# Two graph layers in fp32 on one core: the seven products of a block-matrix unit in three PSUM banks instead of five

## The chip, the cores and the metric

One Trainium2 chip, of which the kernel uses one core. The metric is the device time in microseconds of one execution; the profile is one further execution of the same program, recorded by the hardware profiler. All arithmetic is fp32.

## The reference, cut to what matters

64 graphs of 256 nodes with 512 features pass through two layers that share one 256x256 adjacency matrix. Layer 0 is masked multi-head attention (8 heads of 64), layer 1 a graph attention with one score per pair of nodes. Each layer normalises its input, clips it at zero and adds its result to the input.

```
h = jnp.maximum(_layernorm(x, axis=-1), 0.0)
# layer 0
q, k, v = ((h @ W + b).reshape(b, n, H, HD) for W, b in ...)
scores = jnp.einsum('bqhd,bkhd->bhqk', q, k) / jnp.sqrt(jnp.float32(HD))
scores = scores + (1.0 - adj)[None, None, :, :] * -1000000000.0
out = jnp.einsum('bhqk,bkhd->bqhd', softmax(scores), v).reshape(b, n, d)
x = x + out @ Wo + bo
# layer 1
h = jnp.maximum(_layernorm(x, axis=-1), 0.0)
g = jnp.einsum('bnc,cf->bnf', h, W)
e = leaky_relu(s1[:, :, None] + s2[:, None, :], 0.2) * adj     # s1, s2 = g @ a1, g @ a2
x = x + elu(einsum('bij,bjf->bif', softmax(e), g) + beta * g)
```

## The kernel before, in words

The graphs are worked through in 32 **pairs**. The five matrix products with a 512x512 weight (queries and keys, values, output projection, layer 1) are taken over the two graphs of a pair and over two halves of the weight, as a 2x2 block product with seven block products instead of eight (the Winograd form of Strassen). One such set of seven is a `Unit`: `UnitQK` (two per pair, `ua` and `ub`), `UnitV`, `UnitO`, `UnitW`. A product `P1` to `P7` is eight matmuls into one PSUM bank (128x512). The four results of a unit are called by graph and half: (0,0), (0,1), (1,0), (1,1). With U2 = P1+P6 and U3 = U2+P7 they are P1+P2, U2+P5+P3, U3+P4 and U3+P5.

In the kernel before, `Unit.p` gives P1 (`a`), P4 (`d`), P5 (`b`), P6 and P7 (`k`) a bank each; only P2 is added by TensorE into `a`, and P3 into `b`. ScalarE copies P1 into an SBUF tile `u2` (line 278), VectorE adds P6 to it (280) and P7 into `u3` (283). `put11`, `put2` and `put12` write the results: for queries and keys with the bias (364, 369), for values 398 to 405, for the output projection 490 (into the residual tile `y`, to which GpSimd has added U2 or U3 before, `ahead`, 486), for layer 1 through `elu` (599, 600, 609) and `finish` (614, 615). P3 is accumulated into the bank `b` that `put2` reads for (1,1), so P3 follows that read.

The instructions of TensorE, VectorE, ScalarE and GpSimd run in the order in which the program text issues them; each engine works through its own queue in that order. Only SyncE's queue of DMAs is ordered by the framework. The main loop has two functions per pair p: `first_half` (the values of pair p, then for pair p-2 the layer-1 product, for pair p-1 most of the output projection) and `second_half` (its end, the transposes `x_t` of pair p+1, attention of the two graphs, queries and keys of pair p+1). `v_chain` is the start of `first_half` and holds the softmax of layer 1 of pair p-2: scores (`gat_scores`, 528, 530), exponential (535), division (540, 542), transposes (551). `o_blocks` (460), `combine_2` (299) and `combine_4` (303) form the operand sums of a unit. The first pair and the last ones have texts of their own (`start`, `first`, `last`, `end`).

The residual tiles `y` have six buffers. `residual` loads one (467) and GpSimd adds the bias (468). Four belong to pair p-2 until line 609 has read them, two to (0,0) and (1,1) of pair p-1; so the tile (1,0) of pair p-1 takes the buffer that (0,0) of pair p-2 leaves, and the tile (0,1) the one that (1,1) leaves.

```
    BUFS = {"set": 13, "qk": 8, "v": 4, "pt": 8, "x": 4, "y": 6, "e": 2, "eT": 2, "m": 2, "c": 3, "u": 4}
...
        r = Y[g, fh] = blk(tag, f"y_{g}_{fh}")
        nc.sync.dma_start(r, x[g].rearrange("(t p) c -> p t c", p=P)[:, :, fh * N:(fh + 1) * N])
        nc.gpsimd.tensor_tensor(r, r, bo2[:, fh * N:(fh + 1) * N].unsqueeze(1).to_broadcast([P, 2, N]), ALU.add)
```

## Time and profile before

| | |
|---|---|
| device time, median of 3 runs | 2898.32 us (2898.24 to 2899.57) |
| profiled execution | 2898.09 us, span 2896.3 us, granted TensorE clock 0.999 |
| TensorE busy | 2818.8 us, 97% of the span |
| VectorE, ScalarE, GpSimd busy | 70%, 36%, 57% |
| DMA | 110.00 MB, mean 38 GB/s |

The span runs from the first to the last instruction; about 1.8 us of the execution lie outside it. In the views of instructions, a row gives line, engine, operation, the tiles written and read, shape and count, then the busy time and the mean duration of one, then the idle time of the engine just before such instructions and who ended it. In a timeline a row gives start and length in us, and in square brackets the idle time ahead of it and the engine and tile that ended it. PE is TensorE, DVE VectorE, ACT ScalarE, POOL GpSimd, SPq the DMA queue of SyncE. Matmuls overlap in the records: eight of one product start 0.216 us apart and each is shown some 0.38 us long.

### The profile page before, as it was taken

Reading aid. Unit: us, or ns where it says so; the run is one execution under the profiler, and the core shown is the slowest. Engines: PE = TensorE matmul, PEld = TensorE weight load, DVE = VectorE, ACT = ScalarE, POOL = GpSimd, SP = SyncE. Lnnn points to the kernel's source line nnn. Section 1 sums busy time; section 2 is a strip of 40 time slices with the busy share of each in tenths; the row PEclk is TensorE's granted clock in tenths of the full one; section 3 lists DMA queues with packets and bytes.
Section 4 is the critical chain, followed back from the end, with each engine's and each line's share of the span. In section 5 each row is a group of like instructions: output and inputs, shape, how many; then the busy total and the mean of one; then the engine's idle time right before and its main releaser. Section 6 shows DMA issues by size and latency. Waiting matters only on the chain.

```text
span 2896.3 us, 46339 instructions
## 1 busy us (share of the span) xinstructions
PE 2818.8 (97%) x18110; PEld 2344.3 (81%) x18110; DVE 2035.7 (70%) x3678; ACT 1041.7 (36%) x2122; POOL 1647.2 (57%) x1564
## 2 busy tenths in 40 slices
PE   9999999999999999999999999999999999999997
PEld 7788888888888888888888888888888888888875
DVE  6766766677766767666776667776677766677677
ACT  3233333333343333333333333334333333333324
POOL 3655555556464664645555555646466464555574
PEclk9999999999999999999999999999999999999999
DMA  5010011100111001111001110011100111101111
GB/s 150 5 37 23 30 44 44 44 17 28 44 45 45 29 24 37 44 45 36 24 30 44 45 44 17 29 44 45 44 27 25 37 44 44 34 26 30 37 34 41
DMA packets 96479, 110.00 MB, mean 38 GB/s; under 512 B 8576, under 2 KB 79488, under 8 KB 96256
## 3 DMA queue, kind: packets, MB, share of 16 engines
q1 hardware_dynamic: 96256, 106.99, 11.9%
q8 instruction: 145, 2.38, 0.3%
q14 instruction: 78, 0.64, 0.1%
HBM read 73.41 MB, written 33.55 MB: 37 GB/s over the span
## 4 chain that ended last, share of the span: by engine, by line


## 5 line engine op out<-in xcount | busy, mean ns | idle before, releaser
L422 POOL TENSOR_TENSOR pt<-pt,maskT 128x512 f32<-128x512 f32 x512 | 705.8, 1378 | 663.3 <-ACT pt L421 663.3
L424 POOL TENSOR_TENSOR pp<-pt 128x256 f32<-128x256 f32 x512 | 417.1, 815 | 40.1
L421 ACT ACTIVATE pt<-sc 128x512 f32<-128x512 f32 x512 | 257.6, 625 | 473.5 <-PE sc L417 473.5
L446 DVE RECIPROCAL rec<-sm 128x256 f32<-128x256 f32 x128 | 224.3, 1752 | 73.8 <-PE sm L444 73.8
L518 DVE SCALAR_TENSOR_TENSOR pr<-h,war 128x512 f32<-128x512 f32 x256 | 265.4, 1080 | 0.0
L435 PE MATMUL av<-pt,v 128*32 128x256 f32 x4096 | 246.0, 381 | 0.2 <-DVE v L405 0.2
L417 PE MATMUL sc<-qk 64*128 64x256 f32 x2048 | 238.5, 383 | 0.0
L417 PEld LDWEIGHTS sc<-qk 64*128 64x128 f32 x2048 | 193.1, 187 | 46.0 <-issue 13.5
L564 PE MATMUL pz<-eT,h 128*128 128x256 f32 x1024 | 226.8, 379 | 1.9 <-ACT eT L552 1.9
L614 POOL TENSOR_TENSOR o<-o,m 128x512 f32<-128x512 f32 x29 | 37.0, 1275 | 318.2 <-ACT m L600 307.3
L564 PEld LDWEIGHTS pz<-eT,h 128*128 128x128 f32 x1024 | 194.4, 190 | 28.9 <-ACT eT L552 2.6
L435 PEld LDWEIGHTS av<-pt,v 128*32 128x32 f32 x4096 | 126.6, 110 | 98.4 <-issue 21.5
L486 POOL TENSOR_TENSOR y<-y,o_u 128x512 f32<-128x512 f32 x93 | 126.7, 1377 | 90.1 <-DVE o_u L280 82.6
L535 ACT ACTIVATE e<-e 128x256 f32<-128x256 f32 x128 | 52.2, 409 | 322.5 <-DVE e L530 322.5
L468 POOL TENSOR_TENSOR y<-y,bo 128x512 f32<-128x512 f32 x128 | 161.4, 1283 | 0.0
L567 ACT COPY z<-pz 128x512 f32<-128x512 f32 x128 | 74.9, 587 | 190.3 <-PE pz L564 190.3
L542 DVE SCALAR_TENSOR_TENSOR e<-e,grec,betai 128x256 f32<-128x256 f32 x128 | 137.5, 1112 | 2.3
L351 PE MATMUL qk_p<-h,wq_b 128*128 128x256 f32 x512 | 134.7, 386 | 0.2 <-ACT h L328 0.2
L512 ACT ACTIVATE h<-y,nmr_y,rstd_y 128x256 f32<-128x256 f32 x256 | 132.5, 591 | 1.1
L351 PE MATMUL qk_p<-h,wk_t 128*128 128x256 f32 x512 | 131.5, 379 | 0.0
L351 PE MATMUL qk_p<-h,wq_t 128*128 128x256 f32 x512 | 131.5, 379 | 0.0
L351 PE MATMUL qk_p<-s_h,wq_t 128*128 128x256 f32 x512 | 131.4, 379 | 0.0
(171 smaller groups left out, 6082.2 us busy)
## 6 DMA issues: line engine op xcount, KB each, us to landing
x<-in_x_dram SPq DMA_DIRECT2D x128, 256.0 KB, 2.8
y<-in_x_dram SPq DMA_DIRECT2D x128, 256.0 KB, 2.9
out_dram<-o SPq DMA_DIRECT2D x116, 256.0 KB, 2.6
out_dram<-y SPq DMA_DIRECT2D x11, 256.0 KB, 2.1
wq_b<-in_L_gnn_Wq_dram SPq DMA_DIRECT2D x4, 256.0 KB, 5.8
wk_b<-in_L_gnn_Wk_dram SPq DMA_DIRECT2D x4, 256.0 KB, 6.1
wv_b<-in_L_gnn_Wv_dram SPq DMA_DIRECT2D x4, 256.0 KB, 4.9
wo_b<-in_L_gnn_Wo_dram SPq DMA_DIRECT2D x16, 64.0 KB, 2.5
```

What stands on the lines that cost most here:

```text
L351: nc.tensor.matmul(ps[:, j * N:(j + 1) * N], wj[i][:, c, ft * P:(ft + 1) * P], s[i][:, c, :], start=(start and j == 0 and c == 0), stop=(c ...
L417: nc.tensor.matmul(pss[2 * pair + h][:, k * N:(k + 1) * N], qk[hs, 1, k * P:(k + 1) * P], qk[hs, 0, :], start=True, stop=True)
L421: nc.scalar.activation(pt, two(pss[i]), AF.Exp, scale=QSCALE)
L422: nc.gpsimd.tensor_tensor(pt, pt, maskT, ALU.mult)
L424: nc.gpsimd.tensor_tensor(pp, pt[:, 0, :], pt[:, 1, :], ALU.add)
L435: nc.tensor.matmul(ps[i * HH:(i + 1) * HH, s * N:(s + 1) * N], v[:, k, c0:c0 + HH], pts[i][:, k, :], start=(k == 0), stop=(k == NT - 1))
L446: nc.vector.reciprocal(rec, sums[:, :N])
L468: nc.gpsimd.tensor_tensor(r, r, bo2[:, fh * N:(fh + 1) * N].unsqueeze(1).to_broadcast([P, 2, N]), ALU.add)
L512: nc.scalar.activation(h2[t][:, f * N:(f + 1) * N], Y[g, f][:, t, :], AF.Relu, bias=nmr[:, t:t + 1], scale=rstd[:, t:t + 1])
L518: nc.vector.scalar_tensor_tensor(pr, H2[g][t], 1.0, war[:, j, :], op0=ALU.mult, op1=ALU.mult, accum_out=SC[g][:, t, j:j + 1])
L542: nc.vector.scalar_tensor_tensor(e[:, t, :], e[:, t, :], rec[:, t:t + 1], betai[:, (1 - t) * P:(3 - t) * P], op0=ALU.mult, op1=ALU.add)
L564: nc.tensor.matmul(ps[:, f * N:(f + 1) * N], h2[k][:, fs], eT[:, k, :], start=(k == 0), stop=(k == NT - 1))
```

## The change

P1, P6, P7 and P4 are accumulated one after the other into one bank `a`. After P1, P6 and P7 ScalarE copies the running sum into SBUF (`u1`, `u2`, `u3`), and the next of the four products follows that copy. P2 has the bank `c` to itself, P5 and P3 the bank `b`. VectorE's additions of lines 280 and 283 are gone; (0,0) is now P2 plus `u1` on VectorE, and (1,0) is read straight from `a`. The order of the products in a unit becomes 1, 2, 6, 5, 7, then 4 and 3, with products of another unit, or transposes, between; `queries` interleaves the two units of queries and keys. GpSimd's `ahead` of the output projection remains for (0,0) and (0,1). In `first_half`, `o_blocks` stands earlier, and the second pair of residual loads stands after P7 of `UnitW`. The buffer counts stay. `start`, `first`, `last` and `end` are rewritten to the same scheme, the last `UnitW`s lose their variant with sums on ScalarE and GpSimd (`pooled`), and the last unit has P3 in a bank of its own (`p_34`). The core of the diff:

```diff
-            if i in (2, 3):
-                self.mm(i, self.a if i == 2 else self.b, False)
-                return
-            ps = bank(f"{self.name}_p{i}")
-            setattr(self, {1: "a", 4: "d", 5: "b", 6: "k", 7: "k"}[i], ps)
-            self.mm(i, ps, True)
-            if i == 1:
-                self.u2 = blk("u", f"{self.name}_u2")
-                nc.scalar.copy(self.u2, two(ps))
-            if i == 6:
-                nc.vector.tensor_tensor(self.u2, two(ps), self.u2, ALU.add)
-            if i == 7:
-                self.u3 = blk("u", f"{self.name}_u3")
-                nc.vector.tensor_tensor(self.u3, two(ps), self.u2, ALU.add)
+            if i in (1, 2, 5):
+                setattr(self, {1: "a", 2: "c", 5: "b"}[i], bank(f"{self.name}_p{i}"))
+            ps = {1: "a", 6: "a", 7: "a", 4: "a", 2: "c", 5: "b", 3: "b"}[i]
+            self.mm(i, getattr(self, ps), i in (1, 2, 5))
+            if i in (1, 6, 7):
+                u = blk("u", f"{self.name}_u{i}")
+                setattr(self, {1: "u1", 6: "u2", 7: "u3"}[i], u)
+                nc.scalar.copy(u, two(self.a))
...
-        def put11(self):
-            dst, bias = self.new(0, 0)
-            for j in range(2):
-                nc.scalar.activation(dst[:, j, :], self.a[:, j * N:(j + 1) * N], AF.Identity, bias=bias[j])
-
         def put(self, gi, fh, ps, u):
             dst, bias = self.new(gi, fh)
             for j in range(2):
                 nc.vector.scalar_tensor_tensor(dst[:, j, :], ps[:, j * N:(j + 1) * N], bias[j], u[:, j, :],
                                                op0=ALU.add, op1=ALU.add)
 
-        def put2(self):
+        def put11(self):
+            self.put(0, 0, self.c, self.u1)
+
+        def put22(self):
             self.put(1, 1, self.b, self.u3)
-            self.put(1, 0, self.d, self.u3)
+
+        def put21(self):
+            dst, bias = self.new(1, 0)
+            for j in range(2):
+                nc.scalar.activation(dst[:, j, :], self.a[:, j * N:(j + 1) * N], AF.Identity, bias=bias[j])
 
         def put12(self):
             self.put(0, 1, self.b, self.u2)
...
-            nc.scalar.copy(self.new(0, 0), two(self.a))
-
-        def put2(self):
+            nc.vector.tensor_tensor(self.new(0, 0), two(self.c), self.u1, ALU.add)
+
+        def put22(self):
             nc.vector.tensor_tensor(self.new(1, 1), two(self.b), self.u3, ALU.add)
-            nc.vector.tensor_tensor(self.new(1, 0), two(self.d), self.u3, ALU.add)
+
+        def put21(self):
+            nc.scalar.copy(self.new(1, 0), two(self.a))
...
+            if i == 1:
+                self.ahead(0, 0, self.u1)
             if i == 6:
                 self.ahead(0, 1, self.u2)
-            if i == 7:
-                self.ahead(1, 1, self.u3)
-                self.ahead(1, 0, self.u3)
...
-            self.put(0, 0, self.a)
-
-        def put2(self):
-            self.put(1, 1, self.b)
-            self.put(1, 0, self.d)
+            self.put(0, 0, self.c)
+
+        def put22(self):
+
+            nc.vector.tensor_tensor(two(self.c), two(self.b), self.u3, ALU.add)
+            self.put(1, 1, self.c)
+
+        def put21(self):
+            self.put(1, 0, self.a)
...
+            nc.vector.tensor_tensor(two(self.c), two(self.c), self.u1, ALU.add)
+            self.elu(0, 0, two(self.c))
+
+        def put22(self, step=None):
+
+            if not step:
+                self.s22 = blk(self.tag or "c", f"o_{2 * self.pair + 1}_1")
+                nc.vector.tensor_tensor(self.s22, two(self.b), self.u3, ALU.add)
+            self.elu(1, 1, self.s22, self.s22, step)
+
+        def put21(self, step=None):
+            self.elu(1, 0, two(self.a), None, step)
 
         def put12(self):
-            self.elu(0, 1, self.plus(1, self.b, self.u2))
-
-        def put12_finish(self):
-
-            g = 2 * self.pair
-            y = Y.pop((g, 1))
-            v, m, o = (blk("v", f"{c}_{g}_1") for c in "vmo")
+            nc.vector.tensor_tensor(two(self.b), two(self.b), self.u2, ALU.add)
+            self.elu(0, 1, two(self.b))
...
-            if i == 2:
-                u.put11()
-            if i == 5:
-                u.put2()
-            if i == 3:
-                u.put12()
+            {2: u.put11, 7: u.put22, 4: u.put21, 3: u.put12}.get(i, lambda: None)()
+
+    def queries(p, after=lambda i: None):
+
+        ua, ub = UnitQK(p, 0), UnitQK(p, 1)
+        steps = [(ua, 1), (ua, 2), (ua, 6), (ua, 5), (ua, 7), (ub, 1), (ua, 4), (ub, 2), (ub, 6), (ub, 5), (ub, 7),
+                 (ua, 3), (ub, 4), (ub, 3)]
+        for n, (u, i) in enumerate(steps, 1):
+            products(u, i)
+            after(n)
...
         residuals(p - 1, ((0, 0), (1, 1)))
+        o_blocks(p - 1)
         products(uv, 3)
         combine_24(A["z", p - 2])
-        uw = UnitW(p - 2)
-        products(uw, 1, 4, 6)
+        uw, uo = UnitW(p - 2), UnitO(p - 1)
+        products(uw, 1, 2)
         x_stats(p + 1, 0)
         x_stats(p + 1, 1)
-        products(uw, 2, 7)
+        products(uw, 6)
         x_stats(p + 1, 2)
         x_stats(p + 1, 3)
         products(uw, 5)
         uw.finish(0, 0, nc.gpsimd)
-        o_blocks(p - 1)
         x_scales(p + 1)
+        products(uw, 7)
         residuals(p - 1, ((1, 0), (0, 1)))
-        uo = UnitO(p - 1)
         uo.p(1)
-        uw.p(3)
         combine_2(A["o", p - 1])
+        products(uw, 4)
         x_normals(p + 1, 0, 1)
+        products(uo, 2)
         uw.finish(1, 1, nc.vector)
-        uw.put12()
+        products(uw, 3)
         uw.finish(1, 0, nc.vector)
+        uo.p(6)
         x_normals(p + 1, 2, 3)
-        uo.p(4)
         combine_4(A["o", p - 1])
-        uo.p(6)
+        uo.p(5)
         uw.finish(0, 1, nc.vector)
-        products(uo, 2, 7)
+        products(uo, 7)
         return uo
...
-        products(uo, 5)
+        x_t(p + 1)
+        products(uo, 4)
         y_stats_0(p - 1)
-        x_t(p + 1)
         products(uo, 3)
         values(g0)
         combine_24(A["h", p + 1])
         y_stats_1(p - 1)
         y_stats_2(p - 1)
         scores(g1, {(0, 2): lambda: y_scales(p - 1)})
-        ua, ub = UnitQK(p + 1, 0), UnitQK(p + 1, 1)
-        products(ua, 1, 4, 6)
-        y_normal(p - 1, 1)
-        products(ua, 2)
-        y_normal(p - 1, 0)
-        products(ua, 7, 5)
-        y_sums(p - 1, 1, 0, 1)
-        ub.p(1)
-        products(ua, 3)
-        ub.p(4)
-        ub.p(6)
-        ub.p(7)
-        gat_scores(g1 - 2)
-        gat_exp(g1 - 2)
-        y_sums(p - 1, 0, 0)
-        products(ub, 5)
-        y_sums(p - 1, 0, 1)
-        products(ub, 2, 3)
+
+        def between(n):
+            if n == 5:
+                y_normal(p - 1, 1)
+            elif n == 6:
+                y_normal(p - 1, 0)
+            elif n == 7:
+                y_sums(p - 1, 1, 0)
+            elif n == 8:
+                y_sums(p - 1, 1, 1)
+            elif n == 11:
+                gat_scores(g1 - 2)
+                gat_exp(g1 - 2)
+            elif n == 12:
+                y_sums(p - 1, 0, 0, 1)
+
+        queries(p + 1, between)
...
-        uv.p(4)
+        products(uv, 2)
         divide(p - 2)
-        products(uv, 6, 2, 7)
+        products(uv, 6, 5, 7)
         gat_t(2 * p - 3)
         gat_t(2 * p - 4)
-        products(uv, 5)
+        products(uv, 4)
         return uv
```

## The prediction

> **What bounds the kernel now.** I read the busy shares first, then who TensorE waits for, then its timeline over one pair.

> ```profile
> PE 2818.8 (97%) x18110; PEld 2344.3 (81%) x18110; DVE 2035.7 (70%) x3678; ACT 1041.7 (36%) x2122; POOL 1647.2 (57%) x1564
> ...
> PE o_p L384 <- DVE y L490: 25.7, 31, 1.1
> PE qk_p L351 <- DVE qk L369: 22.7, 31, 0.8
> ```

> TensorE is the bound, and two waits recur in every pair, both for VectorE: the whole rest of the list is 22 us. The timeline shows where they are:

> ```profile
> 1411.52 1.03 PE L351 MATMUL qk_p<-h,wk_b 128*128 128x256 f32 x4
> 1413.32 1.13 PE L351 MATMUL qk_p<-s_h,wq_b 128*128 128x256 f32 x4 [0.77 <-DVE qk L369]
> 1414.29 1.03 PE L351 MATMUL qk_p<-s_h,wk_b 128*128 128x256 f32 x4
> 1415.24 1.93 PE L435 MATMUL av<-pt,v 128*32 128x256 f32 x32
> ...
> 1465.99 1.91 PE L326 MATMUL tr<-ident,x 128*128 128x128 f32 x16
> 1468.74 1.99 PE L384 MATMUL o_p<-wo_b,s_o 128*128 128x256 f32 x8 [0.84 <-DVE y L490]
> 1470.66 1.93 PE L435 MATMUL av<-pt,v 128*32 128x256 f32 x32
> ```

> Both are P3, which must follow `put2`'s read of bank `b`. Four matmuls take 0.863 us elsewhere, a product 1.727. From 1411.52 to 1415.24 lie twelve, 2.59 us of work in 3.72: lost 1.13. Sixteen transposes take 1.75 and P3 1.73, so 1465.99 to 1470.66 has lost 1.19. A wait thus costs its idle time and about 0.36 more: 0.16 by which matmuls otherwise overlap, 0.19 of slower restart. Over the run: 22.7 + 25.7 + 62 x 0.36 = 70.7 us. A pair lasts 89.1 us (values start at 1423.35 and at 1512.48); 2.3 of it are these.

> The other queues matter through their order. The stretch that the change rearranges, layer 1 with the output projection:

> ```profile
> 1455.55 0.96 DVE L609 SCALAR_TENSOR_TENSOR o<-o,y 128x512 f32<-128x512 f32 x1
> 1456.54 1.25 SPq L467 DMA_DIRECT2D y<-in_x_dram  x2
> 1459.96 2.50 POOL L468 TENSOR_TENSOR y<-y,bo 128x512 f32<-128x512 f32 x2
> 1464.95 4.24 POOL L486 TENSOR_TENSOR y<-y,o_u 128x512 f32<-128x512 f32 x3 [2.49 <-DVE o_u L280]
> 1461.71 0.57 ACT L599 ACTIVATE m<-w_p 128x512 f32<-128x512 f32 x1
> ```

> The load of the residual (0,1) leaves 0.03 us after line 609 has read (1,1) of the older pair (1456.51 to 1456.54): it waited for that buffer. GpSimd adds the bias and then idles 2.49 us before its first `ahead`. That slack is what the change uses up.

> [...]P6 must wait for the copy of P1 to end, P7 for that of P6, P4 for that of P7; P3's wait for `put2` above is of this kind. [...]the DMA table shows 2.9 for `y`, which I use. [...]609 takes 0.97 with both inputs in SBUF, 0.69 from PSUM.

> **The change part by part.**

> 1. The two P3 waits go. The read of `b` now follows P7, and P3 comes two products (3.45 us) later at the least in queries, and behind the transposes and P4 (3.5 us) in the output projection; the read is done 0.9 to 2 us earlier. -70.7 us.

> 2. The new waits for ScalarE's copies. The matmuls of a product end 0.16 us after the next product could start; hand-over 0.04, copy 0.586 (line 278), hand-over 0.05: 0.84 us, under a covering product of 1.73. So a copy may be 0.89 late, some 0.5 if weight loading is to run ahead. Of ScalarE's queue by place: after the scores its exponentials end 1.54 us into `ua` P1, which needs the copy at 2.0: free. `y_normal` (2.3 us) stands behind `ua` P7's copy; `ub` P1's copy then ends near 12.35 us from the start of `ua`, its P6 is due at 13.9: free. In layer 1 P6's copy stands behind relu and exp of (0,0) and ends 0.8 before P7. Zero where these covers hold; a VectorE that is 1 us late would cost 0.7 a pair here.

> 3. Values. `put11` (0.61 from start to start) now stands ahead of the divisions on VectorE. Those ended 8.63 us into the unit (1431.98); the second transposes, due at 9.4, get theirs at 9.24, and P4, due at 9.83, its copy at 9.75. The margin is under the 0.2 to 0.3 of weight loading. What that costs is seen at the values' P1: its weight loading waits 0.3 us for the row 451 in every pair (10.3 us in 31), and it takes 1.83 us instead of 1.73: 0.1. So 0.1 a pair, 30 pairs: +3. Bounds 0 and 0.4 a pair.

> 4. VectorE loses 280 and 283 and gains `put11`: a unit less for queries, two for values and layer 1, one for the output, 0.69 each. ScalarE gains two copies a unit, 5 x 2 x 0.586 = 5.9 us a pair, from 36% to some 43%. Neither is the bound: nothing.

> 5. The residual (0,1) and the queue behind it. The second residual loads stand after P7, their bias additions ahead of the new `ahead` (0,0), and `put11` of the output unit waits for that. VectorE's queue behind it holds `finish` (1,1) and the sum of (0,1); ScalarE's queue has relu and exp of (0,1) ahead of the copy that P7 of the output unit waits for. The slot comes free only at line 609 of (1,1). With hand-overs of 0.03 to 0.05 and rows of the groups, in us from the start of layer 1's P7:
> P7 ends 1.89; copy 0.59 (2.52); sum L626 0.68 (3.23); relu L599 0.63 (3.89); L609 0.97 (4.89); DMA 2.9 (7.82); bias L468 1.27 (9.12); `ahead` L486 1.38 (10.43); L490 0.69 (11.15); `finish` L614 and sum L592, overlapping a little (12.34); relu 0.58 (12.95); exp 0.63 (13.61); copy 0.57 (14.08); P7 of the output unit at 14.12.
> Seven products stand between the two, so TensorE is there at 7 x 1.727 = 12.09. It waits 2.03 and pays 0.19 for the restart: 2.2 us. `first_half` runs for p = 2 to 30, 29 times: **+64 us**. A landing of 2.7 or of 3.4 and an uncontended 609 (-0.28) move this from 1.7 to 2.7 a pair. What lies behind is not late again: `x_normals` ends before its transposes, and P3 has a unit's rest as cover.

> 6. Moved: `o_blocks` passes `finish` (0,0) on GpSimd, whose stretch there was idle (the additions of the first residuals end at 1441.15, next work 1452.11): nothing. `y_sums` on VectorE moves within the queries; its results are ready 1.4 us before their transposes. Output stores keep their order; the two residual DMAs are in item 5.

> 7. `start` and `first`: the values' P3 wait of 2.37 us (lost 2.7) goes, as `put22` stands ahead of the weight products; `ua` P6 comes at 17.42 instead of 19.25, but its operand ends at 18.83 (+1.6); the wait of 3.1 before `pwa` goes but may return at the output unit's operand sums, behind the same GpSimd queue (0 to 3). I take -2. `last` and `end`: from 2789 on the waits idle 13 us in all; the same chain of scores, exponential, division, transposes, product stays, with less GpSimd and more VectorE work. I take 0, bounds -6 and +6.

> Sum: -70.7 + 3 + 64.4 - 2 = -5. The profiled execution took 2898.09 us, 0.2 below the median: **2893 us**.

> **The rivals.**

> *The repayment of item 5 holds* (likeliest, 60%): 2893, own range 2878 to 2908, from 1.7 to 2.7 a pair and the ends.

> *Most of the gain stays* (12%): the chain of item 5 doesn't reach TensorE, say because the load is early or the additions fall otherwise. For it speaks only that the chain has fourteen steps; against it, the two loads seen leaving 0.03 us after line 609. Without it 2829; with half of it 2861.

> *Slower: ScalarE's queue holds a second copy back* (28%). In layer 1, P7 waits for the copy of U2, behind relu and exp of (0,0), which wait for VectorE's new sum of P2 and `u1`. The slack is 0.5 us after weight loading. From 0.5 on it counts: 1.5 us of VectorE lateness [...] makes 1.0 + 0.19, 29 times 35 us: 2928. Against it: in the pair shown VectorE is idle there for 3.2 us.

> *It doesn't do what it says*: if the products still had separate banks there would be no new waits and no lost ones; the text of `Unit.p` rules this out.

> **How the numbers follow.** A measurement of this kernel can tell some 0.2% (5.8 us) from no change. The likeliest case lies on that edge: of its 60 points about 28 fall to faster, 22 to the same, 10 to slower. The second gives 12 to faster; the third 2 to the same and 26 to slower. Faster 0.40, same 0.24, slower 0.36. The range 2860 to 2936 takes in the half gain and leaves out the rest of the second case and the worst of the third, under 2 in 10.

> **What would show it.** Waits of P3 for lines of `put2` gone from TensorE's list; in their place one row of the output unit waiting for ScalarE's copy, 29 times, near 1.9 us each, and VectorE idle ahead of `put11`'s 490 for GpSimd by 3 to 4 us. Values' P4 idle below 0.2. Wrong: that row absent (second rival), or one of layer 1 waiting for ScalarE 29 times (third). A pair of 89.1 plus or minus 0.5 us would confirm the sum.

## The result, and the profile after

| | before | after |
|---|---|---|
| median of 4 runs each, taken together | 2898.95 us (2898.24 to 2899.78) | 2918.55 us (2914.21 to 2921.25) |
| profiled execution, span | 2898.09, 2896.3 us | 2920.42, 2918.6 us |
| granted TensorE clock | 0.999 | 0.992 |
| TensorE, VectorE, ScalarE, GpSimd busy | 97, 70, 36, 57% | 97, 65, 41, 54% |

The kernel became **slower**: ratio 1.0066, 95% interval 1.0049 to 1.0084, or 19.6 us, where the prediction had 5 us less. The time lies in the range that was given, on the other side of no change.

First the busy shares of after, and from TensorE's list of waits the rows above 2 us:

```profile
PE 2829.9 (97%) x18110; PEld 2359.0 (81%) x18110; DVE 1887.8 (65%) x3399; ACT 1209.1 (41%) x2436; POOL 1589.5 (54%) x1525
...
PE o_p L381 <- ACT o_u L278: 54.9, 30, 2.0
PE pe L169 <- DVE pr L520: 8.8, 5, 3.0
PE o_p L381 <- DVE s_o L294: 7.3, 2, 7.1
PE w_p L381 <- ACT w_u L278: 2.1, 1, 2.1
```

The two rows of P3 are gone. In their place stands one row that recurs in every pair: the output unit's P7 waits for ScalarE's copy, 30 times; the 29 waits inside the pairs last 1.88 us on average. This is the row that the prediction named, at the size that it named. The 7.1 us for `s_o` belong to the first pair. The row for `pr`, the sums ahead of the layer-1 scores, belongs to the last pairs; before had two such waits there, 1.5 us in all:

```profile
PE pe L169 <- DVE pr L518: 1.5, 2, 0.9
```

TensorE is 11 us longer busy with the same 18110 matmuls. That is the first hint that matmuls themselves became slower.

The stretch of layer 1 and the output projection on TensorE's timeline (start, length, [idle ahead <- by whom]), in the pair that answers to the one shown of before:

```profile
1443.72 1.97 PE L381 MATMUL v_p<-wv_t,h 128*128 128x256 f32 x8
1445.53 7.07 PE L566 MATMUL pz<-eT,h 128*128 128x256 f32 x32
...
1461.07 1.89 PE L381 MATMUL w_p<-w_t,s_z 128*128 128x256 f32 x8
...
1471.42 1.89 PE L381 MATMUL o_p<-wo_t,oT 128*128 128x256 f32 x8
1475.20 1.99 PE L381 MATMUL o_p<-wo_t,s_o 128*128 128x256 f32 x8 [1.89 <-ACT o_u L278]
1477.03 1.91 PE L321 MATMUL tr<-ident,x 128*128 128x128 f32 x16
```

1461.07 is layer 1's P7, from which the prediction counted; 1475.20 is the output unit's P7, 14.13 us later. It was predicted at 14.12. The chain behind it, from the timelines of SyncE's queue, GpSimd, VectorE and ScalarE of the same pair:

```profile
1466.06 2.44 SPq L466 DMA_DIRECT2D y<-in_x_dram  x2
```

```profile
1468.95 1.28 POOL L467 TENSOR_TENSOR y<-y,bo 128x512 f32<-128x512 f32 x1 [3.47 <-DMA y<-in_x_dram]
1470.18 1.27 POOL L484 TENSOR_TENSOR y<-y,o_u 128x512 f32<-128x512 f32 x1
```

```profile
1465.00 1.03 DVE L601 SCALAR_TENSOR_TENSOR o<-o,y 128x512 f32<-128x512 f32 x1 [0.69 <-ACT m L595]
...
1471.48 0.69 DVE L488 TENSOR_TENSOR y<-o_p,y 128x512 f32<-128x512 f32 x1 [3.38 <-POOL y L484]
1472.09 0.68 DVE L606 TENSOR_TENSOR o<-o,m 128x512 f32<-128x512 f32 x1
1472.69 0.69 DVE L624 TENSOR_TENSOR w_p<-w_p,w_u 128x512 f32<-128x512 f32 x1
```

```profile
1473.41 0.60 ACT L595 ACTIVATE m<-w_p 128x512 f32<-128x512 f32 x1 [3.73 <-DVE w_p L624]
1474.05 0.63 ACT L596 ACTIVATE m<-m 128x512 f32<-128x512 f32 x1
1474.58 0.57 ACT L278 COPY o_u<-o_p 128x512 f32<-128x512 f32 x1
```

Read in order of time: VectorE's line 601 (609 in before) reads the buffer until 1466.03, the load leaves at 1466.06; GpSimd, idle for 3.47 us, adds the bias when it has landed and only then does `ahead`; VectorE, idle for 3.38 us, does `put11`, `finish` and the sum of (0,1); ScalarE, idle for 3.73 us, does relu, exp, and then the copy for which TensorE stands. Three engines idle one after the other behind one transfer.

**What isn't in that list** is the clock. The mean of 0.992 is made of short stretches at half speed. Here is a pair that has one, first in TensorE's timeline, then in windows (window, length, busy time and count of PE, PEld, DVE, ACT, POOL; then PEclk, DMA share, GB/s):

```profile
661.50 1.89 PE L381 MATMUL o_p<-wo_t,oT 128*128 128x256 f32 x8
665.29 3.63 PE L381 MATMUL o_p<-wo_t,s_o 128*128 128x256 f32 x8 [1.90 <-ACT o_u L278]
668.71 2.01 PE L321 MATMUL tr<-ident,x 128*128 128x128 f32 x16
```

```profile
662.30:665.70 3.40, 1.50 (x7) 0.95 (x6) 2.74 (x5) 2.17 (x4) 0.32 (x1) 0.97 0.22 77
665.75:669.10 3.35, 3.35 (x11) 2.62 (x10) 1.95 (x2) 1.05 (x3) 1.40 (x1) 0.53 0.69 203
669.15:672.50 3.35, 3.35 (x25) 3.12 (x24) 2.70 (x5) 2.36 (x5) 0.00 (x0) 1.00 0.10 31
```

The wait is the same 1.9 us as at 1475.20. But here P7 takes 3.63 us instead of 1.99: in the 3.41 us that follow, the clock is at a half (0.53 in the window, whose edges are not quite its own), then full again. The clock record of after has eight such stretches in the 29 pairs, each 3.413 us long and each directly behind this wait, besides 6.83 us around the end of the 7.1 us wait of the first pair, and 6.83 and 3.41 us in the last pairs, at the two longest waits for `pr` (2.95 and 2.88 us). Before has one, 3.41 us, behind its 3.1 us wait ahead of `pwa`. The end of the span, when TensorE has no work left, is at half clock in both, for 3.6 us in before and 3.7 in after.

| part of the span | before | after | difference | TensorE idle, before and after | difference by half clock |
|---|---|---|---|---|---|
| start to the first values unit | 100.56 | 98.94 | -1.6 | 4.1, 2.0 | 0 |
| the first pair after it | 74.88 | 77.28 | +2.4 | 4.7, 7.1 | +0.4 |
| 29 pairs | 2584.97 | 2601.18 | +16.2 | 46.0, 54.4 | +13.8 |
| from there to the end | 135.89 | 141.19 | +5.3 | 21.2, 23.7 | at most +2.8 |

Idle is the length less the time in which the profile shows TensorE busy. In the 29 pairs the last column is from their lengths: 21 pairs of after last 89.1 to 89.4 us, close to before's 89.14, and 8 last 90.9 to 91.0, 1.73 more each. At the ends it is an estimate. In the first pair TensorE has work in 4.33 of the 6.83 us at half clock, in before in all 3.41; half of the difference is 0.4. At the end, 2.8 is the time that TensorE is longer busy, for whatever reason; in e10, below, this part has one half-clock window fewer and lasts just as long, 141.15 us, because TensorE then waits longer for the next copy (1.26 instead of 0.45 us). **Of 22.3 us the clock makes 14 to 17, nearly all of it in the 29 pairs.** The rest is idle time at both ends, and the wait itself, which gave back what the P3 waits had cost.

### The profile page after: what moved, and what is told of

The parts are those of the page before. It is cut to its first block, busy times and chain, and to the rows that moved or that the text cites. A ratio compares the mean times of both kernels' runs of the same rounds, so it can differ in the third digit from the quotient of the medians.

```text
span 2918.6 us, 46403 instructions
## 1 busy us (share of the span) xinstructions
PE 2829.9 (97%) x18110; PEld 2359.0 (81%) x18110; DVE 1887.8 (65%) x3399; ACT 1209.1 (41%) x2436; POOL 1589.5 (54%) x1525
## 4 chain that ended last, share of the span: by engine, by line
## 5 line engine op out<-in xcount | busy, mean ns | idle before, releaser
L423 POOL TENSOR_TENSOR pp<-pt 128x256 f32<-128x256 f32 x512 | 423.3, 827 | 40.1
L520 DVE SCALAR_TENSOR_TENSOR pr<-h,war 128x512 f32<-128x512 f32 x256 | 241.4, 988 | 10.6 <-ACT h L514 10.6
L278 ACT COPY qk_u<-qk_p 128x512 f32<-128x512 f32 x192 | 111.8, 582 | 322.3 <-PE qk_p L346 319.6
L359 DVE SCALAR_TENSOR_TENSOR qk<-qk_p,bq,qk_u 128x256 f32<-128x256 f32 x192 | 90.8, 473 | 229.2 <-ACT qk_u L278 208.3
L416 PEld LDWEIGHTS sc<-qk 64*128 64x128 f32 x2048 | 193.0, 187 | 46.0 <-issue 13.9
L467 POOL TENSOR_TENSOR y<-y,bo 128x512 f32<-128x512 f32 x128 | 162.8, 1286 | 100.4 <-DMA y<-in_x_dram 100.4
L434 PEld LDWEIGHTS av<-pt,v 128*32 128x32 f32 x4096 | 126.5, 110 | 98.2 <-issue 21.2
L381 PE MATMUL o_p<-wo_t,s_o 128*128 128x256 f32 x512 | 135.2, 411 | 62.2 <-ACT o_u L278 54.9
L381 PEld LDWEIGHTS o_p<-wo_t,s_o 128*128 128x128 f32 x512 | 100.3, 201 | 88.4 <-ACT o_u L278 66.9
L488 DVE TENSOR_TENSOR y<-o_p,y 128x512 f32<-128x512 f32 x128 | 88.5, 691 | 126.2 <-POOL y L484 94.2
L580 DVE TENSOR_TENSOR s_z<-pz,z 128x512 f32<-128x512 f32 x32 | 22.1, 692 | 219.9 <-ACT z L569 219.9
L484 POOL TENSOR_TENSOR y<-y,o_u 128x512 f32<-128x512 f32 x62 | 93.9, 1515 | 125.8 <-ACT o_u L278 125.8
L595 ACT ACTIVATE m<-w_p 128x512 f32<-128x512 f32 x95 | 56.7, 597 | 197.0 <-DVE w_p L624 117.6
```

The costliest lines, as they stand in the source:

```text
L381: nc.tensor.matmul(ps[:, t * N:(t + 1) * N], s[i][:, c, t * P:(t + 1) * P], wj[i][:, c, :], start=(start and t == 0 and c == 0), stop=(c = ...
L416: nc.tensor.matmul(pss[2 * pair + h][:, k * N:(k + 1) * N], qk[hs, 1, k * P:(k + 1) * P], qk[hs, 0, :], start=True, stop=True)
L423: nc.gpsimd.tensor_tensor(pp, pt[:, 0, :], pt[:, 1, :], ALU.add)
L434: nc.tensor.matmul(ps[i * HH:(i + 1) * HH, s * N:(s + 1) * N], v[:, k, c0:c0 + HH], pts[i][:, k, :], start=(k == 0), stop=(k == NT - 1))
L520: nc.vector.scalar_tensor_tensor(pr, H2[g][t], 1.0, war[:, j, :], op0=ALU.mult, op1=ALU.mult, accum_out=SC[g][:, t, j:j + 1])
```

## The experiments

The account leaves three questions. Is the wait of 54.9 us in all really due to the load's place in GpSimd's queue, and what is the change worth without it? Does the clock drop because of the wait's length, or is it a trait of the new kernel or of the chip? And were the P3 waits priced rightly? Each expectation states the theories that it tells apart. Ratios are to the kernel before, run beside on the same chip (2898.9 to 2899.3 us).

**e1: `ahead` before the second residual loads.** In `first_half` of after, two lines change places:

```diff
-        residuals(p - 1, ((1, 0), (0, 1)))
         uo.p(1)
+        residuals(p - 1, ((1, 0), (0, 1)))
```

> In first_half the second pair of residual loads and their bias additions stand behind the first product of the output unit, so that the addition ahead (0,0) on GpSimd no longer waits for them; nothing else differs from the changed kernel. Theory 1 (the load's buffer, item 5 of the prediction, makes the wait, and the wait makes the clock drops): P7 of the output unit no longer waits for ScalarE, a pair takes 86.9 to 87.1 us instead of 89.2, the mean granted clock is back at 0.997 or more, 2918.6 - 29 x 2.15 - 8 x 1.73 = 2842 us (2836 to 2850). Theory 2 (the clock drops come from denser work on the engines, not from the wait): the wait is gone but the clock stays near 0.992 or falls, 2856 or more. Theory 3 (the copies themselves are late, not the load): the wait stays and the time is 2915 to 2920.

Measured 2844.83 us (5 runs, 2844.53 to 2846.54), ratio 0.9815, 0.9801 to 0.9828. The first rows of TensorE's waits in e1:

```profile
PE pe L169 <- DVE pr L520: 8.8, 5, 3.0
PE o_p L381 <- DVE s_o L294: 7.3, 2, 7.1
PE w_p L381 <- ACT w_u L278: 2.1, 1, 2.1
```

and GpSimd's timeline at the place:

```profile
1427.55 1.26 POOL L484 TENSOR_TENSOR y<-y,o_u 128x512 f32<-128x512 f32 x1 [1.92 <-ACT o_u L278]
1428.78 2.56 POOL L467 TENSOR_TENSOR y<-y,bo 128x512 f32<-128x512 f32 x2
```

The recurring row is gone; `ahead` now waits for its own operand only, and the two bias additions follow it. Time and cause are as expected. Every pair lasts 87.09 us, with no drop of the clock in any, and TensorE isn't idle at all in the 29 pairs. (The mean clock is 0.996, a little under the 0.997 that was expected: the half-clock stretches at the two ends are still there.) The load itself leaves 4.65 us after the start of layer 1's P7 instead of 5.00, still only when its buffer comes free; the 0.34 us are line 601, which takes 0.69 us here, where GpSimd is idle meanwhile, instead of 1.03 beside GpSimd's first bias addition, with both inputs in SBUF in either case. What counts is what stood behind the load and moved ahead: `ahead` starts at 5.11 instead of 9.11. So the wait was the place in the queue. What follows for the change: with these two lines in the other order it is worth 54 us.

**e3, e4, e9, e10: the same kernel, with the wait partly filled.** Ahead of the output unit's P7, n transposes of a constant into a bank of their own (n = 16, 8, 4, 2). P7 still waits for the same copy, at the same time; only TensorE's idle time is shorter.

```diff
         uw.finish(0, 1, nc.vector)
+        fill = bank(f"fill_{p}")
+        for i in range(8):
+            nc.tensor.transpose(fill[:, i % 4 * P:(i % 4 + 1) * P], ident, ident)
         products(uo, 7)
```

> The changed kernel with 16 useless transposes of the identity (1.75 us of TensorE) right ahead of P7 of the output unit in each first_half, into a bank that nobody reads. Theory 1: they lie inside the wait, P7 starts at the same time, TensorE's idle time there falls from 1.9 to 0.3 us or less, the clock is back near 0.998 and the time is lower with more work: 2918.6 - 14 = 2904 (2898 to 2908), all pairs 89.1 to 89.3 us. Theory 2 (clock by density of work): clock 0.992 or less, 2916 to 2922. If the wait were not slack at all: 29 x 1.75 = 51 us more, 2969.

> As the last, with 8 transposes (0.87 us), so that about 1.0 us of the wait stays idle. Theory 1 with a limit on the length of one idle stretch: the kernel before had 62 waits of 0.7 to 0.8 us and only one drop of the clock, so 1.0 us should give none or few: 2904 to 2910, clock 0.996 or more. If the sum of idle time counts and not its length in one piece: drops are halved, 2911, clock about 0.995. Theory 2: 2916 to 2922.

> The changed kernel with 4 useless transposes (0.44 us) ahead of P7 of the output unit: about 1.45 us of the wait stay idle, between the 1.0 us that gave no drop of the clock within the pairs and the 1.9 us that gave 8 in 29. Theory 1 (a drop comes when one window of 3.4 us holds enough idle time): if the limit lies above 1.45 us none, 2904; if below, 1 to 5 drops, 2906 to 2913. Theory 2 (drops in proportion to the idle time): 5 to 6 drops, 2913 to 2915.

> The changed kernel with 2 useless transposes (0.22 us) ahead of P7 of the output unit: the wait there keeps 1.6 to 1.8 us of idle time. In the traces so far a window of a fixed grid of 3.413 us lost the clock when it held 1.86 us or more of idle time (1.97 at the most without a drop), and none with 1.46. Theory 1 (a sharp limit near 1.9 us): no drop within the pairs, pairs 89.1 to 89.3 us, 2904 (2902 to 2908). Rival (the chance of a drop grows with the idle time without a limit): 5 to 7 drops, 2913 to 2917.

| transposes | idle ahead of P7, mean | half-clock stretches in the pairs of the trace | median us | ratio and interval |
|---|---|---|---|---|
| 0 (after) | 1.83 | 8 | 2918.55 | 1.0066, 1.0049 to 1.0084 |
| 2 | 1.6 | 0 | 2906.36 (9 runs) | 1.0025, 1.0015 to 1.0035 |
| 4 | 1.4 | 0 | 2905.24 (14 runs) | 1.0022, 1.0014 to 1.003 |
| 8 | 0.9 | 0 | 2904.18 (16 runs) | 1.0019, 1.0012 to 1.0027 |
| 16 | 0.3 | 0 | 2906.73 (8 runs) | 1.0027, 1.0016 to 1.0037 |

The idle times are these rows of the waits of e10, e9, e4 and e3, in this order, divided by the number of times:

```profile
PE o_p L381 <- ACT o_u L278: 47.4, 30, 1.8
```

```profile
PE o_p L381 <- ACT o_u L278: 40.0, 29, 1.5
```

```profile
PE o_p L381 <- ACT o_u L278: 25.9, 30, 1.0
```

```profile
PE o_p L381 <- ACT o_u L278: 2.9, 11, 0.3
```

Useless work of two transposes, about a fifth of a microsecond in every pair, makes the kernel 12 us faster. All four times are within 3 us of what had been expected if a drop needs a certain idle time; drops in proportion to the idle time had been put at 2913 to 2917 for two transposes. That settles the second question for this place: the copy that P7 awaits is as late as ever, to within 0.1 us, the pairs keep their 89 us, and only the drops are gone. Between 2 and 16 transposes the time hardly changes, so in these runs the time doesn't follow the mean idle time; a limit fits them, above 1.76 us, the longest of these waits with two transposes, which no drop followed. With 16 transposes only 11 waits are left: in the other pairs TensorE reaches P7 when the copy is done, which is a little too much work.

**e5: a longer wait in the kernel before.** If the length of a wait is what counts, a longer wait must bring the drops in the old kernel too. In `UnitO.put2` of before, between the two results, VectorE reads the bank twice more, so that P3 of the output projection waits longer:

```diff
             self.put(1, 1, self.b)
+            for _ in range(2):
+                nc.vector.tensor_reduce(junk, self.b, AX.X, ALU.max)
             self.put(1, 0, self.d)
```

> The kernel before with two useless reads of bank b by VectorE (a maximum over 128x512, about 0.6 us each) behind the reading of (1,1) in put2 of the output unit: P3 of that unit then waits about 2.1 us instead of 0.84 in each pair. Theory 1 (a wait of 2 us lets the clock drop whatever the kernel): 31 x 1.25 = 39 us for the wait, and 7 to 12 drops of 1.7 us: 2948 to 2960, clock 0.993 to 0.995. Theory 2 (the drops belong to the changed kernel's load): no drops, clock 0.999, 2937 (2930 to 2943).

Measured 2962.16 us (4 runs, 2944.13 to 2966.49), ratio 1.0197, 1.0169 to 1.0225. The waits of TensorE, and windows around one of them:

```profile
PE o_p L385 <- DVE junk L499: 65.8, 31, 2.5
```

```profile
1419.20:1422.60 3.40, 1.25 (x6) 1.06 (x6) 3.21 (x7) 0.87 (x2) 1.35 (x2) 1.00 0.00 0
1422.90:1426.20 3.30, 3.30 (x27) 1.49 (x29) 1.60 (x3) 0.00 (x0) 0.00 (x0) 0.50 0.00 0
1426.30:1429.70 3.40, 3.40 (x62) 1.84 (x56) 2.17 (x4) 0.00 (x0) 0.00 (x0) 1.00 0.02 5
```

The wait grew from 0.84 to 2.15 us, and the half clock is there, in a kernel that has nothing of the change. The 15 waits from 224 to 1513 us each have a stretch at half clock behind them, and pairs of 92.08 us; the later ones have none, and pairs of 90.45. The wait is the same 2.15 to 2.17 us in both. A drop costs 1.63 us a pair here, the rest over before's 89.14 is 1.31, just what the wait grew. There are 15 drops where 7 to 12 had been expected, and the median is 2 us above the expected range. The four executions differ by 22 us, and their clocks with them (0.996 with 2944.13 us, 0.988 with 2966.49), as they would if the number of drops varied.

**e11: a longer wait in the new kernel.** An extra ScalarE instruction ahead of `uo.p(6)`, to delay the copy that P7 awaits:

```diff
         uw.finish(1, 0, nc.vector)
+        nc.scalar.mul(junk, mhalf, -1.0)
         uo.p(6)
```

> The changed kernel with one useless ScalarE instruction on 128x4 (about 0.2 us) ahead of the copy that P7 of the output unit waits for: the wait grows to about 2.05 us of idle time. Theory 1 (sharp limit near 1.9 us in one window of the grid): about (3.41 - 2.05 + 0.3) / 3.41, half of the pairs, 12 to 17 of 29, now have a drop: 2918.5 + 29 x 0.2 + 6 x 1.73 = 2935 (2926 to 2943, by the phase of the grid). Rival (drops unrelated to the length of the wait): 2918.5 + 6 = 2924 with 8 drops.

Measured 2919.2 us (4 runs, 2916.32 to 2921.37), ratio 1.0067, 1.005 to 1.0084; 2935 had been expected. The wait row says why:

```profile
PE o_p L382 <- ACT o_u L279: 55.3, 30, 2.0
```

The wait did not become longer. On average over the pairs, the extra instruction does hold the copy back by 0.10 us behind exp, but in this run the whole chain ahead of it is 0.10 us earlier: `ahead` starts 9.01 us after the start of layer 1's P7 instead of 9.11. So the copy starts when it did, the mean idle time is 1.84 us where it was 1.83, and there are nine drops instead of eight. As a test of length it says nothing; what it gives is a second trace at the limit.

**e7 and e8: the P3 waits by themselves.** In the kernel before, only the order of the text changes. e7 moves P5 of `ub` ahead of the layer-1 scores:

```diff
+        products(ub, 5)
         gat_scores(g1 - 2)
         gat_exp(g1 - 2)
         y_sums(p - 1, 0, 0)
-        products(ub, 5)
```

> The kernel before, all its sums and banks as they were, with one line moved: P5 of the second queries unit (and with it put2) stands ahead of the layer-1 scores and node sums, so that P3's wait for put2 has 1.7 us more of cover. Theory 1 (each P3 wait costs its idle time and 0.36): that row leaves TensorE's list, 30 x 1.13 = 34 us less, 2865 (2861 to 2869). Theory 2 (the wait hides other slack, so that the gain of taking it away is smaller): 2875 or more.

Measured 2868.31 us (4 runs), ratio 0.9893, 0.9878 to 0.9908. The P3 row of the queries is gone from the waits, the other remains:

```profile
PE o_p L384 <- DVE y L490: 25.7, 31, 1.1
```

A pair lasts 88.12 us, 1.02 less. The prediction had priced this wait at 1.13. Where the 0.11 went is seen in these lines of e7, where P3 waits for nothing:

```profile
1399.42 1.03 PE L351 MATMUL qk_p<-s_h,wq_b 128*128 128x256 f32 x4
1400.29 1.03 PE L351 MATMUL qk_p<-s_h,wk_b 128*128 128x256 f32 x4
1401.24 1.93 PE L435 MATMUL av<-pt,v 128*32 128x256 f32 x32
```

The last four matmuls take 0.95 us until `av` starts, not 0.86. This step of 0.09 us from a product to `av` is there without the wait too, and the prediction had counted it as a part of the wait's cost. e8 adds to e7 that P3 of the output projection stands behind the values' part of attention:

```diff
         x_t(p + 1)
-        products(uo, 3)
         values(g0)
+        products(uo, 3)
```

> As e7_before_queries, and P3 of the output unit stands behind the values of the first graph (4.5 us of cover) in second_half. Theory 1: both rows leave the list, 2898.9 - 70.7 = 2828 to 2832, which is below the changed scheme with its load order mended (2844.8): the three banks would then not be what the gain needs. Theory 2: holding bank b longer brings a new wait for a bank or for the later statistics: 2840 to 2870.

Measured 2867.78 us (4 runs), ratio 0.989, 0.9875 to 0.9905: no more than e7. The waits and the timeline:

```profile
PE sc L417 <- DVE sm L448: 6.2, 29, 0.2
```

```profile
1457.87 1.99 PE L384 MATMUL o_p<-wo_b,s_o 128*128 128x256 f32 x8
1459.80 2.42 PE L417 MATMUL sc<-qk 64*128 64x256 f32 x18
1462.43 1.96 PE L417 MATMUL sc<-qk 64*128 64x256 f32 x14 [0.21 <-DVE sm L448]
```

P3 waits no more, but the 32 matmuls of the scores behind it take 4.52 us instead of 3.65: they start slower, and then wait for a bank that the value sums still hold. A pair lasts 88.09 us. That five banks to a unit leave none to spare for this order fits the wait; the slower start is not explained by it. So in the one order that was tried, reordering alone gets half of the P3 time out of the old kernel; the other half was got only together with the smaller use of banks.

**e6: e1, and the first pair mended.** The first pair's new 7.1 us wait is, by VectorE's timeline of after, this:

```profile
118.60 1.27 DVE L227 TENSOR_SCALAR betai<-ident,beta 128x128 f32<-128x128 f32 x1 [8.91 <-POOL betai L226]
```

VectorE stands 8.91 us at `betai`, behind GpSimd's memset, which is queued behind GpSimd's part of the first pair's attention. e6 issues the memset at the top of the kernel, and moves `put11` of the first output unit behind its operand sums:

```diff
     betai = const.tile([P, 3 * P], F32, name="betai")
+    nc.gpsimd.memset(betai, 0.0)
...
-                nc.gpsimd.memset(betai, 0.0)
...
-        products(uo, 2)
+        uo.p(2)
         products(uv, 3)
         combine_24(A["o", 0])
+        uo.put11()
```

> The kernel of e1_ahead_first with the first pair mended too: the zeroing of betai by GpSimd stands at the top of the program instead of behind the attention of the first pair, and the sum of (0,0) of the first output unit stands behind the operand sums. Theory: TensorE's one wait of 7.1 us for s_o in the first pair shrinks to 1 to 2 us and the half clock there goes or shrinks: 2844.8 - 5.5 - 2 = 2837 (2833 to 2841). Rival: another wait on GpSimd's queue takes its place: 2843 to 2846.

Measured 2837.96 us (5 runs, 2837.15 to 2839.86), ratio 0.979, 0.9776 to 0.9803: faster than both kernels. The wait is 1.5 us at the longest, the first pair takes 69.52 us instead of 77.24, and the half clock behind it is gone (the two edits were not run apart):

```profile
PE o_p L381 <- DVE s_o L294: 1.8, 2, 1.5
```

Not tried: more buffers for `y`, which would move the load itself.

## Why the prediction was wrong

Point by point, by its own items.

**Item 1, the P3 waits: right in kind, a little too dear.** Both rows are gone. e1, which has the change without the new wait, has pairs 2.05 us shorter than before; with the 0.08 of item 3 the P3 waits were worth 2.13 a pair, where 2.28 had been put down. What was too large is the "0.36 more" for each wait. Of its "0.19 of slower restart" only 0.10 is restart; the other 0.09 is the step from a product to `av`, which stays when the wait goes (e7).

**Items 2, 4 and 6, the copies, the engines' loads and the moves: right.** In the pairs TensorE waits for no copy but the one ahead of P7 of the output unit. ScalarE came to 41%, where some 43 had been put down. The change has 15 reads a pair of a bank to which matmuls still add afterwards. In e1, where none of the copies is late, TensorE isn't idle once in the 29 pairs: under a covering product of 1.73 us the reads cost no wait, and one of them, in the values, costs the 0.08 of item 3.

**Item 3, the values: right.** P4 there takes 1445.53 - 1443.72 = 1.81 us instead of 1.73: 0.08, predicted 0.1.

**Item 5, the repaid wait: right in every step but its last term.** From the start of layer 1's P7, in us:

| | predicted | measured |
|---|---|---|
| bias addition starts, the load having landed | 7.82 | 7.88 |
| `ahead` starts | 9.12 | 9.11 |
| `put11` starts | 10.43 | 10.41 |
| relu of (0,1) starts | 12.34 | 12.34 |
| the copy starts | 13.61 | 13.51 |
| P7 of the output unit | 14.12 | 14.13 |

The load was taken at 2.9 us from the DMA table of before; here it is 1468.95 - 1466.06 = 2.89. P7 starts 2.05 us late (predicted 2.03), and the eight matmuls then take 1.83 us, 0.10 more (predicted 0.19, the figure that holds the step to `av`; transposes follow here).

**The term that failed in the pairs is "pays 0.19 for the restart".** It was taken from the old waits of 0.8 us, none of which ever moved the clock. A wait of 1.9 us has a second cost, which that row could not show and for which the prediction has no term: in 8 of 29 pairs 1.73 us of half clock, 0.48 a pair. The wait thus costs 2.15 + 0.48 = 2.63 us instead of 2.22. The prediction had 29 x (-2.28 + 0.10 + 2.22) = +1 for the 29 pairs; they took +16.2, and 13.8 of the 15 us between are clock. The mean pair of 89.70 us lies 0.1 outside what was to confirm the sum. That the wait causes it, and not the new kernel otherwise, is shown from both sides: filled by two transposes the drops go (e10), and in the old kernel a longer wait brings them (e5).

**Item 7, the ends: -2 was wrong, and nearly half of the miss lies here.** With the share of item 1 that lies outside the 29 pairs the prediction had -6.5 there; measured are +6.1. The clock is the smaller part of these 12.6 us, at most 3.2. The rest is waiting: waits worth 6.5 us were to go at the ends, and TensorE's idle time there grew by 2.8. In the first pair, the wait that "may return ... behind the same GpSimd queue (0 to 3)" did return, at 7.1: the queue was named, but not the memset in it, which stands behind the whole attention of the pair. e6, with its two edits, shows the price: 6.9 us. At the end, "I take 0" rested on "the same chain of scores"; but the waits ahead of the scores' transposes came to 8.8 us in five, where before had 1.5 in two:

```profile
2841.00 0.47 PE L169 MATMUL pe<-ident,s 128*128 128x128 f32 x1 [2.95 <-DVE pr L520]
```

VectorE makes the sums for it one after another there, 1.7 us each. Other waits at the end went, so that TensorE's idle time at the end grew by 2.5 us in all. With +5.3 the end came out near the upper of its "bounds -6 and +6". No experiment changes it, and why it lies there is not shown beyond this.

**The rivals.** The third, ScalarE's queue holding up layer 1's P7, didn't happen: there is no such row, and VectorE had the slack that the prediction saw. The 1.5 us of VectorE lateness in it were the author's estimate, from `combine_24` at 2781.42 in before: 1.16 + 1.65 = 2.81 us, against 0.68 + 0.69 in the pairs. Most of the chance of slower, 26 of 36 points, had been given to it; so the slower result came about without the mechanism that was meant. The second, that most of the gain stays, was out by one exchange of two lines: e1, at 2844.83 where 2829 had been worked out; the ends are most of that difference.

## What to carry to other kernels

A wait of TensorE is not priced by its length alone: where it comes near 2 us on an otherwise dense engine (here 8 of 29 waits of 1.74 to 2.02 us had 3.413 us of half clock behind them, 1.73 us longer a pair, and none of the 29 of up to 1.76 us in e10), look at the granted clock in windows behind it, and shorten the wait or fill it, if need be with useless work. When a step that waits for a transfer is moved in an in-order queue, ask what stands behind it there; here one addition behind a late load held up three engines in turn, and one line put ahead of it was worth 74 us. Take the price of a wait from a wait of its own length: a short one doesn't show what a longer one sets off. And look into the queues of the first and last pairs too: they held nearly half of the miss.

## What the runs showed of the hardware

**The drops of after keep to a fixed grid.** In its pairs they start at 307.1, 665.5, 757.6, 1116.0, 1385.7, 1744.1, 2191.2 and 2372.1 us. The distances are whole multiples of 3.413 us (358.4 = 105 x 3.413, 92.2 = 27 x 3.413), and each of these drops lasts one such window. In the first pair it lasts two; there TensorE still stands idle in the first 2.5 us of the first one.

**In e5 pair length and grid locked.** A pair with a drop lasts 92.08 us, nearly 27 windows (92.16), so the next wait meets the grid at nearly the same place; 15 in a row tripped, as they would until the 0.08 us of drift had carried one over an edge; from there on, at 90.45 us (26.5 windows), no wait of the pairs did. The drops would also account for the spread of after's runs, of which only one has a trace: with clocks of 0.992, 0.993, 0.992 and 0.994 go 2920.42, 2916.68, 2921.25 and 2914.21 us, a range of 7 us, against 1.5 for before, whose recurring waits, 0.84 us at most, are far below 1.86.
